# Four fused graph layers on one core: where the last group's row work stands in the first stripe of a pair layer

## The chip, the core and the metric

The kernel runs on one core of a Trainium2 chip. A core has TensorE (PE, whose weight loads are shown as PEld), VectorE (DVE), ScalarE (ACT), GpSimd (POOL) and the queue engine SyncE (SP). The metric is the device time of one execution in microseconds, as the median of several runs. A profile is one execution, recorded by the hardware.

## The reference, cut to what matters

There are N = 4096 nodes of D = 64 features and a dense 0/1 matrix `adj` of 4096 x 4096. Four layers follow each other, each ending in a layer norm of x plus the layer's result.

```python
# layer 0: mean over neighbours, linear, relu, unit length
h = (adj @ X + X) / (sum(adj, 1) + 1)
z = relu(concat(X, h) @ W + b); out = z / norm(z)
# layers 1 and 3: attention over all pairs in hyperbolic space
x_t = logmap0(x)
adj_att = sigmoid(x_t @ w_l [:, None] + x_t @ w_r [None, :] + b) * adj
support = einsum('ij,ijd->id', adj_att, logmap(x[:, None], x[None, :]))
out = proj(expmap(x, support))
# layer 2: sum over neighbours, weighted by 0.5 ** (neighbours still to come)
out = w @ (x @ weight) + bias
# after each
x = layernorm(x + out)
```

## The kernel before, in words

**Tiling.** The target nodes are cut into four stripes of 1024 (`NW`, `WW`), the same 1024 nodes are also a *group* of eight blocks of 128 (`WB`). `GROUPS` is 3, 2, 1, 0 and `BLOCKS` is 31 down to 0, so group 0 is the last group in everything. A layer goes stripe by stripe, and within a stripe over the 32 source blocks in 16 pairs `g`, each with one load of 1 MB of edges (`load`, tile `edges`, six buffers, SP's queue). So all of `adj` is read once a layer.

**Layer 0.** For each stripe four PSUM accumulators (`sums` twice, `counts` twice, name `acc`, six buffers in pool `m0_ps`) collect `adj @ x` in bf16 parts (L1598). DVE checks on part of the edges that they are 0 or 1 (L886). At the end of a stripe the accumulators are copied to SBUF (L1628, L1636), in the last stripe two by ACT and two by DVE.

**Row work.** What is done once per node is written as Python generators that run in steps between the big instructions. `later` puts one on a queue, `tick(n)` moves time on by n and steps what is due, and a generator yields how many ticks it wants to wait: `soon`, `near`, `after` and `far` work these out; `far(small, large)` counts POOL's small and large operations. `need(tag)` ticks until some generator has finished. For group s after layer 0 the row work is:

- `end_0`: the sums per node (L1544, L1545, PE, into an auxiliary bank `aux` and, where there is one, a spare bank), division by the degree (L1550 to L1553), relu (L1557), squares on POOL (L1559), the norm (L1561, L1562).
- `norm_rows`: mean (L939, L940), variance (L951, L953), one over its root.
- `prepare`: 1 - c |x|^2 and its reciprocal (L974, L977), `y`; then its second half, `second()`: casts into `ys` and `yd` (L986 to L1002), the factor of the logarithm (L1015 to L1053, root `rt`), four transposes (L1040, copied by L1044 into `hi_lo`, `src`, `lo_hi`, `dst`), the products with the attention vectors (L1057), `left` and `right` (L1080 to L1082), and some checks (`good`).

For the last group (`pooled`) most small operations run on POOL. `Small(True, "").rsqrt` is one DVE step (L787) and some ten POOL steps (L791 to L802). ACT takes its logarithms with two activations (L1052, L1053).

**Pair layers (1 and 3), `attend`.** For each block j and stripe s three matmuls per half fill a PSUM tile `z` of two banks, three buffers (L1170, L1173, L1176); ACT makes a sigmoid from `left_b` and `right` (L1190) and a square (L1193); DVE multiplies (L1196, one per block) and combines (L1199, one per two blocks); PE adds up over j (L1148). The accumulator is copied out by L1211. The first stripe of layer 1 begins while group 0 still lacks its row work: `end_0(0)` is queued at its start, and `need((layer, 2 * g // WB))` holds the program order back when the stripe reaches the blocks of group 0, its last four pairs `g`. In layer 3 the same happens behind `end_2`. In the first stripe a block pair has 6 ticks in layer 1 (`rate` 2) and 12 in layer 3 (`rate` 4).

**Order.** In layers 0 and 2 PE and ACT issue in the order in which the program is written (`manual_schedule`). Otherwise a planner in the compiler picks, by its own costs, among what it takes to be ready, in program order. `add_manual_dep` ties one instruction's place in the order behind another's, without a wait. In all but the first stripe of a layer `mark` ties row work on PE, ACT and DVE behind the pairs written before it (`pairs_last`). In first stripes nothing ties it.

Of the kernel before, what the change touches and what calls it, by code (L numbers as in the profile page):

```python
# [10 lines left out]
F32 = mybir.dt.float32  # L11
# [50 lines left out]
def gnn_stack_kernel(  # L62
# [509 lines left out]
    def stream(fits):  # L572

        with ExitStack() as st:
# [23 lines left out]
            pairs_last, seen, anchored = {}, [0], [False]  # L598

            def mark(rows):  # L600
                traced = nc.cur_bb.bb.instructions
                for i in traced[seen[0] :]:
                    if i.engine not in ROW_ENGINES:
                        continue
                    if not rows:
                        pairs_last[i.engine] = i
                    elif anchored[0] and i.engine in pairs_last:
                        tc.add_manual_dep(
                            i, pairs_last[i.engine].name,
                            mybir.DependencyInfo(  # L610
                                mybir.DependencyClass.NoSync, mybir.DependencyReason.DATA
                            ),
                            reason="row work behind the pairs",
                        )
                seen[0] = len(traced)

# [319 lines left out]
            def norm_rows(layer, s, v, x2_to):  # L936

                m, v2, sq = nums("n_m"), nums("n_v2"), grp("sq")
                V.tensor_reduce(m, v, AX.X, ALU.add)  # L939
                V.tensor_scalar(m, m, 1.0 / D, None, ALU.mult)  # L940
                pooled = s == GROUPS[-1]
                E = nc.gpsimd if pooled else V
# [8 lines left out]
                V.tensor_reduce(v2, sq, AX.X, ALU.add)  # L951
                yield soon()
                V.tensor_scalar(m, v2, 1.0 / D, 1e-5, ALU.mult, ALU.add)  # L953
                if pooled:
                    r = yield from Small(True, "").rsqrt(m, "n_r", 0)
                else:
# [8 lines left out]
            def prepare(layer, s, att, b_att, curve, least, good, small):  # L965
# [11 lines left out]
                V.reciprocal(rbg, bg)  # L977
# [7 lines left out]
                def second():  # L985
                    nc.scalar.copy(ys[:, :, :D], y)  # L986
# [27 lines left out]
                    q, q1, t = nums("q"), nums("q1"), nums("tt")  # L1014
                    V.tensor_scalar(q, x2[:, at], least, c, ALU.max, ALU.mult)  # L1015
                    V.tensor_scalar(q1, q, SMALL, None, ALU.max)
                    if pooled:
                        rt = yield from Small(True, "").rsqrt(q1, "rt", 0)
                    else:
                        rt = rsqrt(q1, "rt")  # L1020
# [33 lines left out]
                    yield from free()  # L1054
                    p = take(F32, P, WB, 7)
# [868 lines left out]
```

## Time and profile before

| | |
|---|---|
| median of 3 runs | 1049.47 us (1048.6 to 1050.73) |
| the profiled execution, its own time | 1051.42 us |
| its span, first to last instruction | 1049.7 us |
| PE, DVE, ACT, POOL busy | 977.7, 907.8, 751.7, 322.1 us |
| granted PE clock, mean | 0.986 |
| layer 0, until PE's last sums | 0 to 176 us |
| layer 1, first stripe's end (L1211) | 280.7 us |
| layer 1, second and third | 356.5 and 435.3 us |
| layer 3, the four stripes' ends | 798.6, 875.7, 953.9, 1026.7 us |

The page of the profile gives busy times for the whole span, then the span in slices, then the chain of work that ended last and the costliest groups of instructions. Lines of the order of time read: start in us, length in us, engine, line, operation, output and inputs with their shapes, and in square brackets how long the engine had stood before and what ended that. A length is until the result is written, so neighbours overlap.

### The profile page before, as it was taken

Reading aid. Unit: us, or ns where it says so; the run is one execution under the profiler, and the core shown is the slowest. Engines: PE = TensorE matmul, PEld = TensorE weight load, DVE = VectorE, ACT = ScalarE, POOL = GpSimd, SP = SyncE. Lnnn points to the kernel's source line nnn. Section 1 sums busy time; section 2 is a strip of 40 time slices with the busy share of each in tenths; the row PEclk is TensorE's granted clock in tenths of the full one; section 3 lists DMA queues with packets and bytes.
Section 4 is the critical chain, followed back from the end, with each engine's and each line's share of the span. In section 5 each row is a group of like instructions: output and inputs, shape, how many; then the busy total and the mean of one; then the engine's idle time right before and its main releaser. Section 6 shows DMA issues by size and latency. Waiting matters only on the chain.

```text
span 1049.7 us, 13606 instructions
## 1 busy us (share of the span) xinstructions
PE 977.7 (93%) x4845; PEld 397.9 (38%) x4845; DVE 907.8 (86%) x1401; ACT 751.7 (72%) x873; POOL 322.1 (31%) x695
## 2 busy tenths in 40 slices
PE   5999997979999999999999999998999999999991
PEld 2455554423333333333333344443333333333330
DVE  7486978789999999999488579858999999999996
ACT  0003123769989888898677688888998898888970
POOL 0011111163055365365210020104501662572660
PEclk9999999999999999999999999999999999999996
DMA  8999999655665566566599998996465666665600
GB/s 339 421 416 407 394 422 381 228 189 177 235 233 203 206 240 208 193 241 229 213 327 353 369 358 308 327 332 231 168 233 199 241 210 205 241 229 186 233 1 24
DMA packets 38580, 271.62 MB, mean 259 GB/s; under 512 B 4710, under 2 KB 4710, under 8 KB 5734
## 3 DMA queue, kind: packets, MB, share of 16 engines
q1 hardware_dynamic: 37728, 270.03, 70.0%
q8 instruction: 40, 0.66, 0.2%
q10 hardware_dynamic: 774, 0.63, 0.2%
q14 instruction: 38, 0.31, 0.1%
HBM read 269.58 MB, written 1.05 MB: 258 GB/s over the span
## 4 chain that ended last, share of the span: by engine, by line
PE 60%; DVE 22%; DMA 6%; POOL 5%; ACT 4%; issue 2%; ACTq 0%; SPq 0%; POOLq 0%; DVEq 0%
PE acc L1148 16%; PE z L1790 11%; PE z L1170 8%; DVE t L1199 7%; PE z L1176 7%; PE z L1173 7%; DVE t L1196 6%; DMA edges<-in_adj_dram 5%; PE z L1802 3%; DVE junk L886 3%; PE acc L1598 3%; PE z L1756 2%; ACT sq L1193 2%; ACT sq L1797 1%; DMA w_twice<-in_L_gnn_weight_dram 1%
## 5 line engine op out<-in xcount | busy, mean ns | idle before, releaser
L1196 DVE SCALAR_TENSOR_TENSOR t<-z,sig 128x1024 f32<-128x1024 f32 x256 | 308.6, 1218 | 24.9 <-ACT sq L1193 22.7
L1193 ACT ACTIVATE sq<-z 128x1024 f32<-128x1024 f32 x256 | 255.5, 1023 | 66.0 <-PE z L1176 31.9
L1199 DVE SCALAR_TENSOR_TENSOR t<-sq,t 128x2048 f32<-128x2048 f32 x127 | 294.5, 2319 | 0.3
L1190 ACT ACTIVATE sig<-left_b,right 128x1024 f32<-128x1024 f32 x256 | 287.0, 1149 | 1.9 <-DVE t L1196 1.0
L1148 PE MATMUL acc<-t,xe 128*64 128x512 f32 x1024 | 255.7, 605 | 16.0 <-DVE t L1199 14.7
L1170 PE MATMUL z<-edges,two_i 128*128 128x512 bf16 x512 | 201.1, 393 | 1.1 <-DVE t L1196 1.1
L1176 PE MATMUL z<-dst,src 74*128 74x512 f16 x512 | 195.1, 381 | 0.0
L1173 PE MATMUL z<-lo_hi,hi_lo 128*128 128x512 f16 x512 | 194.0, 379 | 0.0
L1797 ACT ACTIVATE sq<-z 128x512 bf16<-128x512 f32 (+1 forms) x192 | 138.0, 740 | 39.9 <-PE z L1790 38.7
L1148 PEld LDWEIGHTS acc<-t,xe 128*64 128x64 f32 x1024 | 63.6, 136 | 145.0 <-issue 104.3
L886 DVE SCALAR_TENSOR_TENSOR t<-edges 128x2048 bf16<-128x2048 f32 x36 | 82.4, 2304 | 19.7 <-DMA edges<-in_adj_dram 19.5
L1598 PE MATMUL acc<-edges,first 128*128 128x512 bf16 x256 | 80.2, 394 | 20.5 <-DMA edges<-in_adj_dram 20.0
L1170 PEld LDWEIGHTS <-two_i 128*128 128x128 bf16 x512 | 50.4, 98 | 119.9 <-issue 74.7
L1790 PE MATMUL z<-edges,pass_by 128*128 128x512 bf16 x248 | 86.6, 389 | 6.3 <-ACT sq L1797 5.7
L1790 PE MATMUL z<-edges,enter 128*128 128x512 bf16 x256 | 88.3, 387 | 0.0
L1598 PE MATMUL acc<-edges,third 128*65 128x512 bf16 x256 | 79.5, 391 | 0.0
L1176 PEld LDWEIGHTS <-src 74*128 74x128 f16 x512 | 49.2, 96 | 72.6 <-issue 10.6
L886 DVE SCALAR_TENSOR_TENSOR junk<-edges 128x2048 bf16<-128x2048 f32 x28 | 64.0, 2284 | 11.7 <-DMA edges<-in_adj_dram 11.6
L1173 PEld LDWEIGHTS <-hi_lo 128*128 128x128 f16 x512 | 50.3, 98 | 56.6 <-issue 11.3
L1299 POOL TENSOR_TENSOR w_att<-x,u 128x512 f32<-128x512 f32 x6 | 16.2, 2707 | 149.5 <-ACT u L1293 149.5
L1756 PE MATMUL z<-sq,halves 128*128 128x512 bf16 x128 | 48.0, 377 | 0.2 <-ACT sq L1797 0.2
L1404 ACT COPY x_t<-aux 64x512 f32<-64x512 f32 x8 | 4.6, 576 | 57.5 <-PE aux L1399 57.5
(476 smaller groups left out, 989.4 us busy)
## 6 DMA issues: line engine op xcount, KB each, us to landing
edges<-in_adj_dram SPq DMA_DIRECT2D x256, 1024.0 KB, 4.9
x<-in_x_dram SPq DMA_DIRECT2D x4, 256.0 KB
out_dram<-x ACTq DMA_DIRECT2D x2, 256.0 KB
out_dram<-x SPq DMA_DIRECT2D x2, 256.0 KB
w_sb<-in_L_gnn_W_dram ACTq DMA_DIRECT2D x1, 32.0 KB, 4.8
w_twice<-in_L_gnn_weight_dram ACTq DMA_DIRECT2D x2, 16.0 KB, 7.9
given<-in_L_gnn_b_dram ACTq DMA_DIRECT2D x1, 0.2 KB
given<-in_L_gnn_bias_dram ACTq DMA_DIRECT2D x1, 0.2 KB
```

Source lines behind the costliest of these rows:

```text
L886: V.scalar_tensor_tensor(junk, a, 0.0, a, ALU.not_equal, ALU.not_equal, accum_out=odd[:, n : n + 1])
L1148: it = nc.tensor.matmul(acc[h * D : (h + 1) * D, :], xe[:, j, :], t[:, k, h * W : (h + 1) * W], start=j == BLOCKS[0], stop=j == BLOCKS[-1],)
L1170: nc.tensor.matmul(half, two_i, edge[:, at : at + W], start=True, stop=False)
L1173: nc.tensor.matmul(half, hi_lo[:, of], lo_hi[:, to], start=False, stop=False)
L1176: last = nc.tensor.matmul(half, src[:, of], dst[:, to], start=False, stop=True)
L1190: nc.scalar.activation(sig, left_b, AF.Sigmoid, bias=right[:, j : j + 1])
L1193: nc.scalar.activation(sq[:, k], zp, AF.Square, bias=ROOT + OFF, scale=-1.0 / UNIT)
L1196: V.scalar_tensor_tensor(ts[k][:, k], zp, 0.0, sig, ALU.max, ALU.mult)
L1199: V.scalar_tensor_tensor(t, sq, HIGH**2, t, ALU.add, ALU.mult)
L1598: nc.tensor.matmul(accs[h][:m], lhs[:, j, :], edge[:, at : at + W], start=j == BLOCKS[0], stop=j == BLOCKS[-1],)
L1790: nc.tensor.matmul(z[:, h : h + W], lhs, rhs[:, h : h + W], start=j == BLOCKS[0], stop=True, skip_group_check=True,)
L1797: weighed[0] = nc.scalar.activation(w, z[:, :n], AF.Exp, bias=-(OFF_EDGE + CUT) * LN2, scale=-LN2)
```

## The change

- In layer 0 two accumulator tiles are taken and given back (a one-element memset each) ahead of the first stripe, which turns the rotation of the buffers.
- The first sigmoid of layer 1's first stripe is issued in the last stripe of layer 0, before its last ticks, into a buffer of `lefts`. The one-element sigmoid `turned_on`, which loaded the table there, is gone.
- In the last stripe of layer 0 each pair `g` has 5 ticks, not 4.
- In `end_0`, when it runs in layer 1, the first matmul of each half of the sums per node is tied behind the pair matmuls written before it.
- A context `burst` ties the DVE instructions written in it, for the last group: the first one behind the latest pair step of DVE, and the next three pair steps behind its last one. It stands around the division and relu, the norm, the mean, the variance and the reciprocal. In `end_0` there are longer waits (4 ticks ahead of the division, `far(0, 1)` ahead of the norm); one `soon()` between two steps of the variance is gone.
- The two steps that prepare `rt` (L1015, L1016) stand in the burst with the reciprocal, and `rt` itself is computed at the start of `second()`, ahead of the casts. Ahead of the products with the attention vectors the last group waits 2 ticks more.
- `norm_rows` and `prepare` serve layers 1 and 3, so the bursts in them apply to both.

```diff
+            DVE, ahead = mybir.EngineType.DVE, []
+            def in_order(one, behind):
...
             def mark(rows):
...
                     if not rows:
                         pairs_last[i.engine] = i
+                        if i.engine == DVE and ahead:
+                            in_order(i, ahead.pop())
...
+            @contextmanager
+            def burst(on):
+                traced = nc.cur_bb.bb.instructions
+                start = len(traced)
+                yield
+                ours = [i for i in traced[start:] if i.engine == DVE]
+                if on and ours:
+                    if DVE in pairs_last:
+                        in_order(ours[0], pairs_last[DVE])
+                    ahead[:] = [ours[-1]] * 3
...
+                with burst(pooled):
+                    V.tensor_reduce(m, v, AX.X, ALU.add)
+                    V.tensor_scalar(m, m, 1.0 / D, None, ALU.mult)
...
+                with burst(pooled):
+                    V.tensor_reduce(v2, sq, AX.X, ALU.add)
+                    if not pooled:
+                        yield soon()
+                    V.tensor_scalar(m, v2, 1.0 / D, 1e-5, ALU.mult, ALU.add)
+                    if pooled:
+                        r = yield from Small(True, "").rsqrt(m, "n_r", 0)
...
+                qs = [nums(n + "_0") for n in ("q", "q1")] if pooled else []
+                with burst(pooled):
+                    V.reciprocal(rbg, bg)
+                    if pooled:
+                        V.tensor_scalar(qs[0], x2[:, at], least, c, ALU.max, ALU.mult)
+                        V.tensor_scalar(qs[1], qs[0], SMALL, None, ALU.max)
...
                 def second():
+                    if pooled:
+                        rt = yield from Small(True, "").rsqrt(qs[1], "rt", 0)
                     nc.scalar.copy(ys[:, :, :D], y)
...
                     yield from free()
+                    if pooled:
+                        yield 2
+                        yield from free()
                     p = take(F32, P, WB, 7)
...
+            def sigmoid(layer, s, j):
+                early = layer == 1 and j == BLOCKS[0] and s == GROUPS[0]
+                if early:
+                    sig = lefts.tile([P, WW], F32, name="left_b")
+                else:
+                    sig = sb.tile([P, WW], F32, name="sig", bufs=3)
+                nc.scalar.activation(sig, left_bs[s], AF.Sigmoid, bias=right[:, j : j + 1])
+                return sig
...
+                        sig = ahead_of.pop() if ahead_of else sigmoid(layer, s, j)
...
+                                if place[0] == 1 and not k:
+                                    in_order(one.ins, pairs_last[mybir.EngineType.PE])
...
+                        pooled = s == GROUPS[-1]
+                        if pooled:
+                            yield 4
+                        with burst(pooled):
...
-                    V.tensor_scalar(z, z, 0.0, None, ALU.max)
...
-                    yield 1
-                    V.tensor_reduce(n2, sq, AX.X, ALU.add)
-                    V.tensor_scalar(n2, n2, 1e-24, None, ALU.max)
-                    if s == GROUPS[-1]:
-                        n = yield from Small(True, "").rsqrt(n2, "n", 0)
+                    yield far(0, 1) if pooled else 1
+                    with burst(pooled):
+                        V.tensor_reduce(n2, sq, AX.X, ALU.add)
+                        V.tensor_scalar(n2, n2, 1e-24, None, ALU.max)
+                        if pooled:
+                            n = yield from Small(True, "").rsqrt(n2, "n", 0)
...
+                        if s == GROUPS[0]:
+                            for _ in range(2):
+                                V.memset(ps.tile([P, W], F32, name="acc")[:1, :1], 0.0)
...
-                            tick(4)
+                            if last and g == 0:
+                                ahead_of.append(sigmoid(1, GROUPS[0], BLOCKS[0]))
+                            tick(5 if last else 4)
...
-                        if last:
-                            nc.scalar.activation(turned_on, one_row[:, :1], AF.Sigmoid)
```

## The prediction

> **What bounds the kernel now.** I read the stages first (busy time by window), then the eight times at which a stripe's accumulator is copied out (line L1211), then the waits and the order of time around the worst stage.
>
> ```profile
> 188.00:254.00 66.00, 58.75 (x302) 23.08 (x300) 58.39 (x75) 54.62 (x58) 30.16 (x56) 1.00 0.55 192
> 254.00:281.00 27.00, 26.36 (x120) 9.70 (x119) 25.95 (x21) 26.43 (x29) 0.00 (x0) 1.00 0.61 216
> 281.00:357.00 76.00, 76.00 (x338) 27.09 (x336) 74.99 (x55) 68.21 (x73) 35.20 (x88) 1.00 0.64 223
> ```
>
> Columns after the length: busy us of PE, PEld, DVE, ACT, POOL, then clock and DMA. In a settled stripe (third row) PE is busy all 76 us: PE sets the pace, with DVE close behind. In the first stripe of layer 1 (rows one and two) neither is full. The copies L1211 come at 280.7, 356.5 and 435.3 us, so settled stripes take 75.8 and 78.8 us; the first one takes 280.7 - 183.65 (its first pair matmul) = 97.1 us. In layer 3 the first stripe goes from its first L1196 at 709.0 to 798.6 us, 89.6, and the next takes 77.1. So some 18 us and 12 us lie in the two first stripes, the ones the change touches. Where they go, at the seam:
>
> ```profile
> 176.18 0.34 PE L1057 MATMUL aux<-att,hi_lo 128*128 128x7 bf16 x8
> 180.63 0.66 PE L1544 MATMUL aux<-sum_w,sums 128*128 128x65 f32 x2 [4.11 <-DVE own L1070]
> ...
> 183.65 0.63 PE L1170 MATMUL z<-edges,two_i 128*128 128x512 bf16 x1
> ```
>
> PE stands 4.11 us (the sums per node need an auxiliary bank that DVE still reads), then computes half of those sums, then the first pairs. The first pair step of DVE, L1196, comes at 187.56. And inside the stripe:
>
> ```profile
> 211.00 0.69 DVE L939 TENSOR_REDUCE n_m<-z 128x8 f32<-128x512 f32 x1 [2.26 <-POOL z L1566]
> 211.61 2.28 DVE L1199 SCALAR_TENSOR_TENSOR t<-sq,t 128x2048 f32<-128x2048 f32 x1
> 213.81 0.16 DVE L940 TENSOR_SCALAR n_m<-n_m 128x8 f32<-128x8 f32 x1
> 213.88 1.22 DVE L1196 SCALAR_TENSOR_TENSOR t<-z,sig 128x1024 f32<-128x1024 f32 x1
> 216.31 0.69 DVE L951 TENSOR_REDUCE n_v<-sq 128x8 f32<-128x512 f32 x1 [1.21 <-POOL sq L945]
> ```
>
> The last group's chain of small steps goes back and forth between DVE and POOL. Its DVE links come too early (DVE stands 2.26 and 1.21 us) or are cut by a 2.2 us L1199. Its last link, L1082 `right`, ends at 253.1 us; four of the stripe's sixteen block pairs need it.
>
> **What the Trainium skill says.** "TensorE: Matmul & The Clock Gate", Part 1: after an idle window of about 3.4 us the PE clock is halved, until a similar window of work has passed. The trace agrees: after the 4.11 us the clock is half until about 187.4 us, and start to start of a pair matmul is 0.43 us, not 0.22. "SBUF — State Buffer", section "SBUF: two separate sides": DVE and GpSimd share a port pair as an exclusive lock, which a DVE operation with two SBUF inputs takes for its whole length. The trace fits it: POOL L801 takes 0.20 us at 208.01 and 2.13 at 222.86, beside L1199 (0.196 to 2.279 us over its 23 runs). "ScalarE: Activation LUTs", "What ACT_TABLE_LOAD costs": a load takes 1.283 us; here L1623's took 1.28.
>
> **The change part by part.**
>
> *Rotation.* The banks are those of the program of before. The last stripe of layer 0 sits in banks 2, 5 (`sums`) and 6, 3 (`counts`); the first `z` of layer 1 covers 2 and 3. So it waits for `sums[0]` (ACT) and `counts[1]` (DVE, L1636, ended 179.7). Banks are given out in the order in which they came free; with two taken and returned at the start, I work out 6, 3 and 4, 1: the first `z` waits for one DVE copy, `sums[1]`, the next two for ACT alone. The two memsets cost about 0.06 us each, before x has landed (DVE idles 2.07 us there for it): nothing.
>
> *tick(5).* The row work of group 1 starts its second half 48 ticks into the last stripe: 12 block pairs at four ticks, 9.6 at five. At 2.45 us a pair (edges come at that pace) that is 5.9 us earlier. DVE's run of small steps, from 171.06 to 181.2 with the copies near its end, then ends near 175, and the copies follow PE's last sums (176.0) at once: `sums[1]` by 176.8. Cover: layer 0 waits for edges; transposes that come early could make PE wait, and six load buffers at 2.45 us hide up to about 12 us of that. Cost 0; without the cover 1 us.
>
> *Sums behind the pairs.* The first `z` need not stand behind L1544: 176.8 instead of 183.65. PE idles under 1 us, so the clock stays whole. Six matmuls at 0.22 give the first L1196 at 176.8 + 1.4 = **178.2 instead of 187.56: 9.4 us**. The sixteen small fp32 pairs then follow two `z` (16 x 0.22 = 3.5 us), beside 2 x 1.13 + 2.2 = 4.5 us of DVE work that is ready: nothing, 3.5 us if DVE runs out.
>
> *Early sigmoid.* It takes over the table load (1.28 + 0.20 us at L1623, just ahead of the sums' copies) and one 1.15 us sigmoid, in a stretch where ACT stands 5.84 us for transposes. Nothing is added; the copies start up to 1.5 us earlier, counted above. It waits for `right` and `left_b` of the first group, long done. Behind it in ACT's order stand only copies that wait for PE.
>
> *Bursts and their waits.* The instructions stay; their places become fixed: behind the latest pair step of DVE, and ahead of the next three. The first stripe has 6 ticks a block pair, 72 up to the pair that needs the last group. By the yields of after the chain is: sums at tick 4 to 6, divide and relu +4, norm +7, mean +12, variance +1+8, reciprocal +12, second half +7+1, transposes +13, then two turns of 2, the new 2, and 2: 75 to 79, forced at 72. Before, the same count is about 68, but the trace took 253.1 - 187.56 = 65.5 us, for DVE was not where the plan had it. A pair costs DVE 2 x 1.13 + 2.2 + gaps = 4.54 us, and the small steps some 6 us in twelve pairs: (12 x 4.54 + 6)/72 = 0.84 us a tick. So 178.2 + 72 x 0.84 = 238.7, and about 6 us of links (transposes, copies, Ln with two table loads, products), as the trace took from 247 to 253: `right` near **245, 8 us earlier**. Each link has POOL's time in its wait: variance 9 ticks = 7.6 us for 2.1 us of work, reciprocal 12 = 10 us for 7.2 in the trace with two collisions. So DVE should not stand in a burst. From `right` to L1211 took 27.6 us; four pairs at 4.62 and the drain, with less left over (the turns of group 1 are done by then), I put at 26: **271 instead of 280.7, 9.7 us**. Bounds: no gain if the chain slips by 10 us; 15 us if it never binds, since DVE's own work, 178.2 + 16 x 4.54 + 6 + 3 of drain + 3, ends at 263 to 266.
>
> *rt moved ahead of the copies.* POOL's eleven steps (3.1 us plain, 7.1 in the trace with two collisions) run before rather than behind the copies into `ys`: the Ln at 246.2 waited for them, while the casts wait only for `y`. POOL's later steps (`ys` L996 to L1012, 5 us) come that much later, and the transposes wait for these: 0, between -2 and +3 us. It is inside the bounds above.
>
> *Layer 3.* Same bursts, no new start. There `right` ends at 757.2 and is needed near 775, so the chain does not bind; what can go is DVE's 1.37 us before L977 and some of PE's three waits for L1199 (1.31, 0.62, 1.29). I take **1 us**, between -3 and +3.
>
> Sum: 9.7 + 1 = 10.7 us. The profiled execution took 1051.42 us (span 1049.7), so it would take 1040.7; against the median of 1049.47 shown, **1038.8, say 1039**. What comes after the first stripe is as before: settled stripes are PE's.
>
> **Rivals.** *(a) The chain never binds.* DVE alone sets the first stripe: 15 + 1, so 1033.5. For it: links would have to follow each other as fast as planned. Against: the tick count passes 72.
> *(b) The chain keeps its end.* Earlier start, longer fixed waits: 79 ticks at 0.92 instead of 0.84 bring `right` to 251. Gain 2 + 1: 1046.5. For it: the tick of before was (250 - 187.56)/72 = 0.87.
> *(c) Slower: DVE stands in its bursts.* A burst cannot be passed, so when POOL is late, three pair steps and behind them PE stand. There are five bursts with POOL ahead of them in layer 1 and three in layer 3. Each collision costs POOL 2 us. If the lateness averages above 10.7/8 = 1.3 us a burst, the gain is gone; at 1.9 the time is 1049.5 + 4.5 = 1054. Against: the margins above.
> *(d) The seam does not move.* DVE is still busy with group 1 at 180 and the first `z` waits for its copy. Only the order against L1544 is won, 3 us at half clock: 1046 to 1049.
>
> **How the numbers follow.** Chances: forecast 0.50 (1034 to 1044), (a) 0.14, (b) 0.17, (d) 0.07, (c) 0.12. Leaving out the tails of (a) and (c) gives 1030 to 1049. A measurement of this kernel can tell about 0.2%, 2.1 us, from no change. Faster: forecast, (a), most of (b) and half of (d), 0.82; same 0.07; slower (c), 0.11.
>
> **What would show it.** The first pair matmul near 177 with no half clock at the seam; first L1196 near 178; L1082 of the last group near 245; the first L1211 near 271 and the first of layer 3 about 90 us after its start, or 1 less; 2 us stalls of DVE gone ahead of L939 and L977. It is wrong if the seam is right and L1211 still comes at 278 or later (then b or c: look for DVE waiting for POOL at L1561, L939, L951, L977), or if layer 3's first stripe grows.

## The result, and the profile after

The change makes the kernel slower. Its median is 1059.48 us (1058.44 to 1061.62, 5 runs), beside 1050.40 us for the kernel before (1048.6 to 1051.96): a ratio of 1.0089, 95% interval 1.0075 to 1.0103. The profiled execution spans 1057.4 us, 7.7 more than before (1049.7). Its lines L1223, L1226, L1229, L1241, L1181 are L1193, L1196, L1199, L1211, L1148 of before; L1166 is the sigmoid, L1082 and L1083 are the two Ln.

The busy time by window, with the windows moved to the changed kernel's own stages (columns as before: busy us of PE, PEld, DVE, ACT, POOL, clock, DMA):

```profile
186.00:254.00 68.00, 56.76 (x270) 22.40 (x275) 63.24 (x78) 52.13 (x54) 29.84 (x56) 0.98 0.58 216
254.00:283.00 29.00, 28.02 (x129) 10.54 (x130) 21.01 (x17) 27.12 (x29) 0.00 (x0) 0.94 0.52 181
283.00:360.00 77.00, 76.51 (x338) 27.66 (x343) 76.23 (x57) 69.51 (x74) 35.38 (x88) 1.00 0.65 224
```

In the first row DVE is now busy 63.2 of 68 us (before 58.4 of 66): the first stripe up to `right` is nearer to DVE's bound, yet not shorter. In the second DVE falls to 21.0 of 29 us; before it had 26.0 of 27.

The stages, in us. *First step* is the first pair step on DVE (L1226), *right* the end of the last group's `right`. The last three columns are kernels of the experiments below. Each column is one execution: those of e5 and e8 took 2.3 and 0.5 us more than their medians, that of e11 2.7 us less.

| | before | after | e5 | e8 | e11 |
|---|---|---|---|---|---|
| PE's last sums of layer 0 end | 175.9 | 179.8 | 175.9 | 174.7 | 175.1 |
| first z on PE | 183.65 | 182.88 | 180.59 | 182.20 | 177.44 |
| first step | 187.56 | 185.72 | 184.48 | 186.10 | 180.42 |
| `right` | 253.2 | 254.1 | 252.6 | 252.0 | 245.3 |
| first stripe's sums copied | 280.7 | 283.0 | 278.8 | 277.6 | 271.1 |
| second stripe takes | 75.8 | 77.1 | 77.2 | 77.2 | 75.7 |
| layer 3, first stripe, from first step | 89.6 | 93.1 | 90.35 | 90.4 | 90.7 |
| pair steps on DVE ahead of `right` | 23 | 24 | 24 | 24 | 24 |
| DVE idle from first step to `right` | 7.05 | 4.31 | 4.12 | 2.18 | 1.95 |

So the 7.7 us are 2.3 up to the end of the first stripe, 1.4 in the second, 3.6 in layer 3's first and 0.8 in its other three, less 0.3 elsewhere. Three places of the trace carry it.

**The seam.** The order of time of PE, then of ACT, in the changed kernel:

```profile
170.41 0.62 PE L1070 MATMUL aux<-ident,ys 128*128 128x128 f16 x8 [2.71 <-DVE ys L1031]
...
180.06 0.61 PE L1070 MATMUL aux<-ident,yd 128*74 128x128 f16 x8
182.88 0.39 PE L1203 MATMUL z<-edges,two_i 128*128 128x512 bf16 x1 [2.21 <-ACT w_att L1679]
```

```profile
179.81 1.15 ACT L1166 ACTIVATE sig<-left_b,right 128x1024 f32<-128x1024 f32 x1 [3.04 <-DVE lr L1100]
180.87 0.99 ACT L1074 COPY lo_hi<-aux 128x1024 f16<-128x1024 f16 x1
181.76 0.59 ACT L1671 COPY sums<-acc 128x512 f32<-128x512 f32 x1
182.24 0.59 ACT L1679 COPY w_att<-acc 65x512 f32<-65x512 f32 x1
```

Three pairs before the end of layer 0 PE stands 2.71 us for a row step of group 1, which the fifth tick put ahead of the remaining pairs; at 151.5 us it had stood 1.09 for another row step. The two, 3.8 us together, are the bulk of the 3.9 us by which layer 0 ends later (some 0.7 us of transposes and products that stood behind the last sums now stand ahead of them too, and about 1 us of waits for edges falls away), for nothing hides them: in this stripe PE waits for no edges from 136.8 us on, as in the kernel before from 133.6 to 168.3 (there it then waits 0.53 and 0.51 us for them, without any wait for row work). Then the first z waits for ACT: a second sigmoid stood 3.04 us for group 1's row work, and behind it in ACT's order are `lo_hi` and only then the copies of the sums. The half clock at the seam is gone in this execution (z matmuls follow at 0.22 us), and from the last sums to the first step it is 5.9 us instead of 11.7. Net, the first step is 1.8 us earlier. In the second profile of this kernel (e9) z matmuls follow at some 0.43 us from 183.7 to 186.3, and the first step comes at 187.2, only 0.4 us earlier than before.

**Inside the stripe.** DVE in the changed kernel, the bursts and what stands after them:

```profile
211.20 0.69 DVE L960 TENSOR_REDUCE n_m<-z 128x8 f32<-128x512 f32 x1
...
218.79 0.68 DVE L972 TENSOR_REDUCE n_v<-sq 128x8 f32<-128x512 f32 x1
...
239.73 0.23 DVE L1097 TENSOR_SCALAR m<-b,k_of_y 128x8 f32<-128x8 f32 x1 [2.01 <-POOL xe L1041]
...
258.74 1.23 DVE L1226 SCALAR_TENSOR_TENSOR t<-z,sig 128x1024 f32<-128x1024 f32 x1 [4.57 <-ACT sig L1166]
```

L960 and L972 (before L939 and L951) carry no brackets any more: the 2.26 and 1.21 us are gone, as the bursts intend. New are 2.01 us for POOL, which runs `rt` first and so reads the old `m` later, and 4.57 us for a sigmoid. That last wait does not come from the table loads of the next paragraph alone: kernels with the bursts and only two loads still have 2.6 to 3.2 us of it (e2, e5 to e8, e11, e12), and those without bursts (before, e3, e4, e10) have none.

**The logarithms.** ACT in the changed kernel, squares and sigmoids left out, and under it the same stretch of the kernel before:

```profile
240.22 1.28 ACT L1082 ACT_TABLE_LOAD   x1
244.29 0.21 ACT L1082 ACTIVATE tt<-tt 128x8 f32<-128x8 f32 x1 [2.79 <-POOL tt L1052]
...
245.43 1.28 ACT L1166 ACT_TABLE_LOAD   x1
...
248.69 1.00 ACT L1074 COPY hi_lo<-aux 128x1024 f16<-128x1024 f16 x1
249.71 1.28 ACT L1083 ACT_TABLE_LOAD   x1
251.00 0.21 ACT L1083 ACTIVATE q<-q 128x8 f32<-128x8 f32 x1
...
256.27 1.28 ACT L1166 ACT_TABLE_LOAD   x1
```

```profile
237.85 1.01 ACT L1044 COPY hi_lo<-aux 128x1024 f16<-128x1024 f16 x1
...
244.72 1.28 ACT L1052 ACT_TABLE_LOAD   x1
246.23 0.21 ACT L1052 ACTIVATE tt<-tt 128x8 f32<-128x8 f32 x1 [0.22 <-POOL tt L1022]
...
247.25 0.20 ACT L1053 ACTIVATE q<-q 128x8 f32<-128x8 f32 x1
247.46 1.28 ACT L1190 ACT_TABLE_LOAD   x1
```

Before, the planner put `hi_lo` first, then both Ln between one table load and one back. In the changed kernel the first Ln stands ahead of `hi_lo`: ACT loads the table, stands 2.79 us for POOL, and goes back to the sigmoid's table; after `hi_lo`, copied 10.8 us later than before, the second Ln needs a load of its own and a fourth brings the sigmoid back. PE meanwhile runs dry (busy 2.08 of 5.7 us from 246.0) and its clock is 0.56 in the 6.8 us from 251.7. Layer 3 has the same four loads, at 745.0, 749.1, 756.3 and 759.5 us, with 1.71 us for POOL and `hi_lo` at 752.4 instead of 745.4. I call this *the split Ln*.

### The profile page after: what moved, and what is told of

The parts are those of the page before. It is cut to its first block, busy times and chain, and to the rows that moved or that the text cites. A ratio compares the mean times of both kernels' runs of the same rounds, so it can differ in the third digit from the quotient of the medians.

```text
span 1057.4 us, 13525 instructions
## 1 busy us (share of the span) xinstructions
PE 974.0 (92%) x4760; PEld 399.0 (38%) x4845; DVE 909.3 (86%) x1403; ACT 758.0 (72%) x876; POOL 317.5 (30%) x695
## 4 chain that ended last, share of the span: by engine, by line
PE 54%; DVE 15%; ACT 5%; issue 1%; POOL 1%; ACTq 0%; POOLq 0%; DVEq 0%
PE acc L1181 16%; PE z L1833 11%; PE z L1206 7%; DVE t L1229 7%; PE z L1209 7%; PE z L1203 6%; DVE t L1226 6%; PE z L1845 3%; PE z L1799 2%; ACT sq L1223 2%; ACT sq L1840 1%; PE aux L1312 1%; ACT sig L1166 1%; PE aux L1147 1%; PE aux L1070 0%
## 5 line engine op out<-in xcount | busy, mean ns | idle before, releaser
L1226 DVE SCALAR_TENSOR_TENSOR t<-z,sig 128x1024 f32<-128x1024 f32 x255 | 306.6, 1217 | 27.4 <-ACT sq L1223 20.6
L1223 ACT ACTIVATE sq<-z 128x1024 f32<-128x1024 f32 x256 | 255.2, 1021 | 64.0 <-DVE t L1229 28.6
L1229 DVE SCALAR_TENSOR_TENSOR t<-sq,t 128x2048 f32<-128x2048 f32 x127 | 296.3, 2333 | 0.5
L1166 ACT ACTIVATE sig<-left_b,right 128x1024 f32<-128x1024 f32 x255 | 286.0, 1149 | 6.3 <-DVE lr L1100 3.0
L1181 PE MATMUL acc<-t,xe 128*64 128x512 f32 x1024 | 257.2, 611 | 15.6 <-DVE t L1229 15.0
L1203 PE MATMUL z<-edges,two_i 128*128 128x512 bf16 x463 | 180.9, 391 | 5.7 <-DVE t L1226 3.5
L1181 PEld LDWEIGHTS acc<-t,xe 128*64 128x64 f32 x1024 | 64.2, 137 | 145.0 <-issue 106.9
L1833 PE MATMUL z<-edges,enter 128*128 128x512 bf16 x248 | 85.9, 387 | 0.5
L1799 PE MATMUL z<-sq,halves 128*128 128x512 bf16 x122 | 45.7, 377 | 0.5 <-ACT sq L1840 0.2
```

The lines of the kernel that those rows point to most:

```text
L1166: nc.scalar.activation(sig, left_bs[s], AF.Sigmoid, bias=right[:, j : j + 1])
L1181: it = nc.tensor.matmul(acc[h * D : (h + 1) * D, :], xe[:, j, :], t[:, k, h * W : (h + 1) * W], start=j == BLOCKS[0], stop=j == BLOCKS[-1],)
L1203: nc.tensor.matmul(half, two_i, edge[:, at : at + W], start=True, stop=False)
L1223: nc.scalar.activation(sq[:, k], zp, AF.Square, bias=ROOT + OFF, scale=-1.0 / UNIT)
L1226: V.scalar_tensor_tensor(ts[k][:, k], zp, 0.0, sig, ALU.max, ALU.mult)
L1229: V.scalar_tensor_tensor(t, sq, HIGH**2, t, ALU.add, ALU.mult)
```

## The experiments

All ratios are to the kernel before, run beside each group on the same chip (medians 1050.3, 1049.5 and 1049.9 us), with 95% intervals. Single executions of these kernels scatter by up to some 10 us, and the longer ones have the lower granted clock (in e1 the fastest of 12 took 1050.8 us at a mean of 0.988, the slowest 1064.1 at 0.975); so the medians tell the size and the profiles the place.

| run | kernel | median us | ratio |
|---|---|---|---|
| e9 | changed kernel again | 1058.24 | 1.0077 (1.0056 to 1.0098) |
| e1 | changed, four ticks | 1057.32 | 1.0069 (1.0046 to 1.0092) |
| e2 | changed, Ln together | 1051.91 | 1.0016 (1.0002 to 1.0029) |
| e3 | changed, no bursts | 1060.36 | 1.0106 (1.0077 to 1.0136) |
| e4 | before, seam's edits alone | 1055.60 | 1.0057 (1.0036 to 1.0078) |
| e5 | e2 and four ticks | 1048.90 | 1.0001 (0.9988 to 1.0015) |
| e6 | e5, ScalarE's copies | 1047.89 | 0.9989 (0.9977 to 1.0002) |
| e7 | e5, short waits | 1048.17 | 0.9986 (0.9968 to 1.0004) |
| e8 | before, row work's edits, Ln together | 1051.09 | 1.0019 (1.0009 to 1.0029) |
| e10 | e4 with four ticks and ScalarE's copies | 1050.59 | 1.0008 (0.9996 to 1.0020) |
| e11 | e5, ScalarE's copies and short waits | 1045.12 | 0.9960 (0.9945 to 0.9976) |
| e12 | e11, layer 3's row work as before | 1043.35 | 0.9942 (0.9922 to 0.9961) |

My theory from the result's trace was: the split Ln and the fifth tick make the loss. The main rival: the bursts with their fixed places do.

### The two Ln together (e2), and the changed kernel again (e9)

```diff
-                        nc.scalar.copy(into[:, cols], turned[:n])
+                        turns_made.append(nc.scalar.copy(into[:, cols], turned[:n]))
...
-                        nc.scalar.activation(t, t, AF.Ln, bias=1.0)
-                        nc.scalar.activation(q1, q1, AF.Ln, bias=1.0, scale=-1.0)
+                        one = nc.scalar.activation(t, t, AF.Ln, bias=1.0)
+                        two = nc.scalar.activation(q1, q1, AF.Ln, bias=1.0, scale=-1.0)
+                        if pooled:
+                            in_order(one.ins, turns_made[0].ins)
+                            in_order(two.ins, one.ins)
```

`turns_made[0]` is the copy of `hi_lo`. So the tie does two things, which no run takes apart: it keeps the two Ln together, and it lets `hi_lo` go first.

> The changed kernel with one tie more in the last group's row work: the first Ln is issued on ScalarE behind the copy of hi_lo, and the second behind the first with only the copy of src and one square between them, so that each first stripe has one table load for Ln and one back, where the changed kernel has two of each. Theory (the planner set the first Ln ahead of hi_lo's copy, where ScalarE stood 2.8 us for POOL in layer 1 and 1.7 us in layer 3, and split the two Ln): hi_lo is copied some 8 us earlier, two loads of 1.28 us go in each first stripe, the first stripe of layer 1 goes from 97.3 us (first pair step to the copy of the sums) to 91 to 94, that of layer 3 from 93.1 to 89 to 91, and the whole is 5 to 9 us shorter: 1050 to 1054 us. Rival (the chain is bound by POOL's and VectorE's links, and ScalarE's wait only moves): right is written within 1 us of where it is now in both stripes, and the whole is 0 to 3 us shorter: 1056 to 1059 us.

> The changed kernel once more, beside the others of this study on one chip. It should be 0.7 to 1.0% slower than the kernel before, and 0.6 to 0.8% slower than the kernel with both Ln tied alone if the tie's gain of 7.6 us is real; if the two were only measured on different chips, it comes out within 0.3% of the kernel before.

Measured: 1051.91 us, and the changed kernel beside the last group again 1.0077. The tie is worth 0.61 to 0.73% of the time, 6.4 to 7.7 us: the theory's side. Layer 3 shows it plainly. ACT there in e2, squares and sigmoids left out:

```profile
750.33 1.00 ACT L1076 COPY hi_lo<-aux 128x1024 f16<-128x1024 f16 x1
...
753.19 1.28 ACT L1084 ACT_TABLE_LOAD   x1
754.49 0.21 ACT L1084 ACTIVATE tt<-tt 128x8 f32<-128x8 f32 x1
...
755.50 0.21 ACT L1085 ACTIVATE q<-q 128x8 f32<-128x8 f32 x1
755.72 1.28 ACT L1171 ACT_TABLE_LOAD   x1
```

There are two loads, and the first stripe falls from 93.1 to 90.3 us. It takes 90.3 to 90.7 us in every profile with the tie there (e2, e5 to e8, e11) and 93.1 to 94.8 in all with the split (after, e9, e1, e3).

In layer 1 the profiles don't settle the size. This execution of e2, the slowest of its 22 (1057.7 us), had layer 0 end at 182.4 us and half clock at the seam, and its stripe took 96.7 us, as the rival wanted, with `right` 70.5 us after the first step. e5, which has the same tie, takes 94.3 us. With the split it is 97.3 us in the changed kernel, and 95.7 in e9, which has the same four loads in both stripes. So the profiles show 2.8 us in layer 3 and at most some 3 in layer 1; the rest of the medians' difference lies in executions of which there is no profile.

### Four ticks in layer 0's last stripe (e1), and both mends (e5)

```diff
-                            tick(5 if last else 4)
+                            tick(4)
```

> The changed kernel with one edit undone: tick(4) again after each pair of layer 0's last stripe; rotation, early sigmoid, sums behind the pairs, bursts and the rt move stay. Theory (the fifth step brings row work of group 1 in front of the last pairs, and TensorE stands 2.7 us at 170.4 us for a VectorE copy three pairs before the end, too late to catch up): the last sums of layer 0 end within 1 us of the kernel before (176.0 us, against 179.8 in the changed kernel), the first stripe of layer 1 keeps its 97 us, and the whole is 3 to 4 us shorter than the changed kernel: 1055 to 1057 us, ratio to the kernel before near 1.005. Rival (layer 0 ends later because of the swapped banks or the sigmoid in ACT's fixed order, or only because the loads ran behind): the last sums still end near 179 us and the whole stays within 1 us of 1059.5. Second rival (group 1's row work then falls into the first stripe of layer 1 and pushes that one back): layer 0 ends near 176 us, but the stripe behind it takes 100 us and the whole is unchanged.

> The changed kernel with both Ln of the last group tied together behind the copy of hi_lo, and with four ticks again in layer 0's last stripe. If the split Ln (7.6 us of the medians) and the fifth step (2.2 us) add up, the whole is 1049 to 1050.5 us, no slower than the kernel before; layer 0 ends near 175.7 us and layer 3's first stripe takes 90 us. Rival (the fifth step's time is paid back at the seam, where the sums' VectorE copies then stand behind group 1's row work and the first z waits 4 us for them): 1051.5 to 1053 us, as with the tie alone.

Measured: in e1 layer 0 ends at 175.7 us, so the fifth tick is what made it late (the five profiles with it end layer 0 at 179.4 to 182.4 us; of the nine with four ticks eight end it at 174.7 to 175.9, e7's at 178.1). But the second rival has a part too: e1's PE, then its DVE, at the seam:

```profile
180.40 0.61 PE L1203 MATMUL z<-edges,two_i 128*128 128x512 bf16 x1 [4.04 <-DVE u L1679]
```

```profile
178.98 0.17 DVE L1111 TENSOR_TENSOR f<-f,m 128x8 f32<-128x8 f32 x1
179.07 0.68 DVE L1671 COPY sums<-acc 128x512 f32<-128x512 f32 x1
179.67 0.68 DVE L1679 COPY u<-acc 65x512 f32<-65x512 f32 x1
```

This profile is the slowest of e1's 12 (1064.1 us), but e5's has the same wait (4.05 us). Group 1's row work now ends at 179, DVE's two copies of the sums stand behind it, and the first z waits 4.04 us. Most of what layer 0 gains is lost again, and that idle time brings back the half clock. The whole is 1057.3 us, 0.9 to 2.2 us below the changed kernel's two medians, and the intervals overlap: alone it is not shown to help. With the tie as well (e5) it is 1048.9 us, 0.1 below the range expected: by the ratios 1.6 us below e2 and 8 to 9 below the changed kernel. The loss is gone, ratio 1.0001.

### The bursts: taken out of the changed kernel (e3), and the row work's edits without the seam's (e8)

e3 replaces `with burst(pooled)` by `with burst(False)` and takes back `yield 4` and `far(0, 1)`. e8 has tie, bursts, waits and the `rt` move, and none of the seam's edits.

> The changed kernel with the bursts and the longer waits that came with them undone (each small VectorE step is issued where the kernel before had it, far(0,1) is 1 again and the 4 ticks behind the sums per node go); rotation, fifth step, early sigmoid, sums behind the pairs, rt ahead of the copies and the 2 ticks ahead of the products stay. In layer 1 the copies of hi_lo and src stand ahead of both Ln in ScalarE's order, with one load each way; in layer 3 the Ln stay split by four loads. Theory (the split Ln and ScalarE's wait for POOL make the stripes longer, not the bursts): layer 1's first stripe falls from 97.3 to about 92 us, layer 3's stays at 93, and the whole is 4 to 6 us shorter than the changed kernel: about 1054 us. Rival (the bursts themselves, with their longer waits and POOL's operations thrown beside the large VectorE steps, make both stripes longer): both stripes come back to the kernel before, 93 and 89.5 us, and the whole is 7 to 8 us shorter: about 1052 us. Third case (the bursts did help as predicted and something else hides it): both stripes grow by 5 us or more, and the whole is 1065 us or more.

> The kernel before with the row work's edits alone (bursts and their waits, rt ahead of the copies, 2 ticks ahead of the products) and both Ln tied together; no rotation, four ticks, no early sigmoid, sums per node in the kernel before's place. If the bursts bring what the idle time of VectorE ahead of right allows (7.05 us in layer 1's first stripe of the kernel before, of which the changed kernel has 4.3 left; 4.3 against 4.0 us in layer 3), less the one pair step by which right stands later: layer 1's first stripe 91 to 94 us, layer 3's 90.3, the whole 1048 to 1051 us, no change against the kernel before. Rival A (the bursts and waits are a loss by themselves, and the seam's edits a gain that hides it): 1053 us or more. Rival B (the seam's edits are the loss, 5.3 us when they were made alone, and the bursts a gain): 1046 us or less.

Measured: e3 is 1060.4 us; none of its three cases. Its two stripes took 97.8 and 93.4 us. In layer 1 the Ln do stay together and `hi_lo` is copied at 236.3 us, but DVE stands 12.1 us ahead of `right` instead of 4.3, and ACT stands 3.44 us for POOL between the table load and the first Ln. So without the bursts the chain is longer by itself, and taking them out of this kernel wins nothing. Layer 3 shows which edit splits the Ln where: bursts gone, four loads still, from 743.1 to 757.4 us. There the split comes from what e3 keeps: the `rt` move, the two ticks ahead of the products, or the `soon()` that is gone; in layer 1 it comes with the bursts or their longer waits, which e3 takes out together. With none of these (e4) both stripes have two loads.

e8 is 1051.1 us, 1.0019: between its cases, nearest the first. The bursts take DVE's idle time ahead of `right` from 7.05 to 2.18 us. But `right` now stands behind 24 pair steps and 12 of the large step that combines them (L1229 of the changed kernel), where it stood behind 23 and 11, and the large one takes 2.39 us each instead of 2.28. So `right` comes 65.9 us after the first step, as before (65.7). The first stripe wins 1.7 us, the second gives back 1.4 and layer 3's first 0.8.

### The seam's edits alone (e4), and mended (e10)

e4 is the kernel before with rotation, fifth tick, early sigmoid and the tie of the sums per node. e10 has four ticks and the mended copies of e6 below.

> The kernel before with the edits at the seam alone: rotation, fifth step in layer 0's last stripe, early sigmoid, sums per node behind the first pairs; no bursts, rt and q where they were, no ticks ahead of the products. Theory: layer 0 ends near 179.8 us as in the changed kernel (the fifth step), the first pair steps follow 6 us later, near 186, and since both Ln stay together the first stripe of layer 1 takes about as long as before plus the few us by which the row work of the last group now starts later against the first pair step: 93 to 97 us; layer 3 is as before, 89.6 us; the whole is 0 to 3 us from the kernel before: 1048 to 1053 us. Rival (the seam's gain of 5.6 us can never be kept, because the last group's chain sets the end of the stripe and starts with the sums): the copy of the first stripe's sums lands 3 to 4 us later than before, at 284 us, whatever the first pair step gained, and the whole is 1053 to 1055 us.

> The kernel before with the seam's edits alone (rotation, early sigmoid, sums per node behind the first pairs), four ticks, and the last sums copied by ScalarE alone; row work as in the kernel before, both Ln together by the planner's own order. Theory (of the 5.3 us that the seam's edits cost alone, layer 0's late end made some 5 and VectorE's wait for POOL the rest, 13.5 us idle ahead of right against 7.1): first pair step near 180.5 us instead of 187.2, and the whole 1048 to 1051 us. Rival (with the seam's edits POOL's steps fall beside VectorE's large ones whenever the first step comes, and eat what was won): VectorE's idle time ahead of right stays at 12 us or more, the first stripe takes 98 us or more, and the whole is 1050 to 1053 us, though the first step comes 7 us earlier than in the kernel before.

Measured: e4 1055.6 us, the rival's side, for two reasons. Layer 0 ends at 180.8 us, so the first step comes at 187.15, hardly earlier than before (187.56). And the stripe from there takes 98.5 us instead of 93.2. DVE in e4, then POOL in e4:

```profile
211.52 0.69 DVE L960 TENSOR_REDUCE n_m<-z 128x8 f32<-128x512 f32 x1 [4.01 <-POOL z L1596]
...
229.78 0.20 DVE L1000 RECIPROCAL rb<-b 128x8 f32<-128x8 f32 x1 [2.23 <-POOL b L996]
```

```profile
198.10 2.95 POOL L1587 TENSOR_TENSOR sq<-z 128x512 f32<-128x512 f32 x1 [26.37 <-DVE z L1582]
...
205.41 2.20 POOL L816 TENSOR_SCALAR rs_t<-rs_t 128x8 f32<-128x8 f32 x1
```

POOL's squares take 1.04 us alone and 2.95 here, beside DVE's large step; its small step 0.24 and 2.20. Between 196 and 227 us five POOL steps are held so in e4, one in the kernel before. DVE waits 13.5 us ahead of `right` instead of 7.05. But held steps alone do not decide: the changed kernel has four between 196 and 227 us, and no wait of DVE stands ahead of its bursts.

In e10 the first step comes at 180.9 us, 6.6 earlier than before, and yet the time is the same, 1.0008: it is not the late end of layer 0 alone that eats the gain. Its profiled execution is one of its slowest (1056.4 us; median 1050.6). DVE stands 18.7 us in it, 4.3 of them in 13 us of half clock behind the seam (0.53 by the windows) and 6.8 in its waits for POOL ahead of the mean, the variance and the reciprocal (4.8 before); `right` ends at 257.2 us, 4 later than before. So the rival's numbers for DVE and the stripe (103.6 us) came, and the earlier start brought nothing. Its mechanism did not come: five POOL steps up to `right` are held in e10, as many as before, and one of them between 196 and 227 us. That the phase against DVE's large steps decides in e4 is a reading of its trace; no run changed the phase alone, and for e10 the cause stays open.

### Mends: ScalarE's copies (e6), short waits (e7), both (e11), and layer 3 as before (e12)

```diff
-                            copy = V.tensor_copy if last and h else nc.scalar.copy
+                            copy = nc.scalar.copy
...
-                        if pooled:
-                            yield 4
...
-                    if pooled:
-                        yield 2
-                        yield from free()
```

The first line is e6's, the others e7's; e11 and e12 have all. e12's bursts, `rt` move and tie are in layer 1 alone.

> As the kernel with both Ln tied and four ticks, and the two VectorE copies of layer 0's last sums go to ScalarE too, so that they stand behind no row work. Theory (the first z waits for the copies: 4.04 us for VectorE with four ticks, 2.21 us for ScalarE with five): layer 0 ends near 175.7 us, the first z starts near 178 us instead of 180.4, the first pair step falls from 184.3 to about 181.5 us, and the whole is 2 to 3 us below that kernel, 1046.5 to 1048.5 us. Rival (the last group's chain, placed by ticks, and the row work of group 1 set the end, so the first pair step alone brings nothing): first z near 178 us, but TensorE or VectorE stands for group 1's row work a step later, and the whole is within 1 us of that kernel.

> As the kernel with both Ln tied and four ticks, without the two waits that were added by count: the 4 ticks between the sums per node and their use, and the 2 ticks ahead of the products of the last group. Theory (in ticks, right stands behind the 24th pair step of layer 1's first stripe where the kernel before had it behind the 23rd, and the chain is as long as its ticks): right moves one or two pair steps forward, to 22 or 23, the stripe is 2.5 to 5 us shorter, layer 3's first stripe 1 us, and the whole 3 to 5 us below that kernel: 1045 to 1047 us. Rival (without the waits VectorE stands in the bursts for TensorE and POOL instead): right at the 23rd step but VectorE's idle time ahead of it grows by 3 us or more from 4.3, and the whole is within 1 us of that kernel or above it.

> The changed kernel with both Ln tied, four ticks, ScalarE's copies and without the two waits by count. If the gains of the copies (0.12%) and of the shorter waits (0.15%) add up: 1045 to 1047.5 us, 0.2 to 0.4% below the kernel before. If the first pair step no longer matters because VectorE stands for the last group's sigmoid afterwards (3.2 us with the short waits): 1047.5 to 1048.5 us.

> As the mended kernel (both Ln tied, four ticks, ScalarE's copies, without the two waits by count), and layer 3's first stripe with its row work as in the kernel before: no bursts, rt behind the copies, no tie. There the stripe takes 89.6 us instead of 90.4, so the whole should be 0.5 to 1 us below the mended kernel, 1044 to 1047 us: bursts cost layer 3 0.8 us. If bursts cost nothing there, the two are equal.

Measured: e6 has the first z at 177.21 us and the first step at 180.25, even earlier than its theory said, and is 1.0 us below e5, as its rival said (the intervals overlap): in the profiles `right` moves from 252.6 to 250.8 us only. In e7 the second stripe falls to 75.7 us, so its 1.4 us more came from the waits by count; the first takes 92.4. The whole is 1048.2 us, a smaller gain than expected; in its profile layer 0 ends at 178.1. `right` stands behind the 24th step here too, with no new wait for POOL ahead of it: the step count does not come from these waits. Together (e11) they give 1045.1 us, 0.40% below the kernel before: by the medians more than the sum of the two, though the intervals don't tell it from the sum. The windows of e11 for the first stripe, and its ACT, PE and DVE at the seam:

```profile
180.40:245.00 64.60, 60.68 (x312) 24.93 (x317) 62.16 (x76) 54.97 (x58) 31.92 (x56) 1.00 0.63 233
245.00:271.00 26.00, 25.55 (x113) 9.31 (x113) 22.66 (x20) 25.44 (x27) 0.00 (x0) 1.00 0.63 218
```

```profile
175.89 0.60 ACT L1679 COPY u<-acc 65x512 f32<-65x512 f32 x1
176.36 1.03 ACT L1076 COPY src<-aux 74x1024 f16<-74x1024 f16 x1
177.27 2.21 ACT L1168 ACTIVATE sig<-left_b,right 128x1024 f32<-128x1024 f32 x2
179.36 1.95 ACT L1225 ACTIVATE sq<-z 128x1024 f32<-128x1024 f32 x2
```

```profile
177.44 0.39 PE L1205 MATMUL z<-edges,two_i 128*128 128x512 bf16 x1 [1.73 <-ACT src L1076]
```

```profile
180.42 1.23 DVE L1228 SCALAR_TENSOR_TENSOR t<-z,left_b 128x1024 f32<-128x1024 f32 x1 [2.12 <-ACT sq L1225]
```

The clock is whole in both windows, DVE is busy 62.2 of 64.6 us, and the first stripe's sums are copied at 271.1 us: the number that the prediction had for the change. That execution took 1042.4 us, though, and e11's median is 1045.1. e12 has the same program up to there; its profile, with half clock for part of the time behind the seam (0.87 from 181 to 194 us, e11's is whole), has its first step at 180.5 and the copy at 274.4. e12 is the fastest, 1043.35 us, ratio 0.9942, against 1.0089 of the change. Its layer 3 takes 89.6 us where e11's takes 90.7. That layer 3 is better without the bursts and the other row edits is shown by the profiles (89.6 us in all four without them: before, e4, e10, e12); by the medians it is not, since the intervals of e11 and e12 overlap.

## Why the prediction was wrong, point by point

The forecast was 10.7 us shorter, with 11 in 100 for slower; the trace is 7.7 longer, the median 9.1. Of the 18.4 us between, 12.0 lie ahead of the first L1241 (271 predicted, 283.0 measured), 1.4 in the second stripe, 4.6 in layer 3's first (1 less predicted, 3.6 more measured), the rest behind it. In the forecast's own terms, the gain was to come almost all from the seam (9.4 us, of which 1.8 came), and the loss came mainly from a term put near nothing, the order on ACT: two table loads were assumed, four came, and the tie alone takes the loss from 0.77 to 0.89% back to 0.16%.

- **tick(5), "Cover ... Cost 0; without the cover 1 us": failed.** I took it that layer 0 waits for edges, and the load buffers for a cover of PE's waits. But in the last stripe the trace of before has no wait for edges from 133.6 to 168.3 us: PE was behind them, and full buffers don't give a late PE its time back. What could be hidden was the 1 us of its two waits at the end; the row steps cost 1.09 and 2.71 us, and layer 0 ended 3.9 us late. (With four ticks, e1 and e5: 175.7 and 175.9 us.)
- **Rotation and early sigmoid, "the first `z` waits for one DVE copy" and "only copies that wait for PE": failed.** z waited for ACT. I looked at what stands behind the early sigmoid, not at the next sigmoid, which stood 3.04 us for group 1 ahead of the copies. I had 2.2 us from last sums to first step; it was 5.9. With copies that stand behind nothing (e6, e11) it is still 5.3: the first z comes 2.35 us after the sums instead of 0.8, behind one more copy of ACT (`src`), and the first step 3.0 us after the first z instead of 1.4. That is a link which I had left out: DVE's step waits until ACT's square has ended, as the last fence above shows.
- **Sums behind the pairs:** right in that PE no longer stands for them. That the clock stays whole at the seam came in this profile and not in e9's. The size was 1.8 us instead of 9.4, for the two reasons above: 7.5 us of the 12. That the first z can come by 177 was true, once ScalarE alone makes the copies: 177.44 in e11, 6.2 us earlier than before.
- **Bursts, 0.84 us a tick:** this part of the sum was nearly right. From first step to `right` I had 66.8 us, and 68.4 was measured; the twelve L1229 took 2.39 us each where L1199 took 2.28, which is 1.3 us of the difference. But 66.8 is more than the 65.7 of before: the sum itself said that bursts lengthen the chain, and all its gain came from the seam. I did not read that off. (The terms of its tick count add to 77 to 79, not 75 to 79; the chain was taken as forced at 72 all the same.) The stalls that they take away are small, 4.9 us of 7.05 in e8, and there the extra pair step and the longer L1229 cost the same.
- **"About 6 us of links ... Ln with two table loads", and rt "0, between -2 and +3": failed.** Four loads. I followed POOL's order and took ACT's as given, but outside layers 0 and 2 the planner chooses it anew, and a moved step can change it far from the edit. The split Ln costs 6.4 to 7.7 us by the medians, most of the loss: with the tie alone (e2) the change is 1.0016, and with four ticks as well (e5) 1.0001. From `right` to the copy I had 26 us; it was 28.9, with 4.57 us of DVE waiting for a sigmoid and 6.8 us of half clock, and 26.6 in e9. e11 has 25.9.
- **Layer 3, 1 us shorter:** 3.6 longer. 2.8 are the split Ln (e5: 90.35) and 0.8 the bursts with the rest of the row edits (e12: 89.6). The range I gave, -3 to +3, was too narrow by half a microsecond.
- **Rival (c)** had the sign, not the mechanism: DVE stands nowhere in a burst. The places that I named for it (ahead of the norm, the mean, the variance, the reciprocal) show no wait. **(b)**, `right` near 251 by longer waits, is nearer (254.1). The waits by count do cost: 1.4 us in the second stripe.
- **What would show it wrong** said: if layer 3's first stripe grows. It did, and it is the cleanest sign, as no edit at the seam reaches it (89.6 us in e4 and e10, as before).

## What to carry to other kernels

When an edit moves one step in a program whose order a planner chooses, read the new order of every engine before costing it, first where an engine pays to change state: two activations of one table that fall apart here cost two loads of 1.28 us, a wait between them and what stands in line behind. The Trainium skill's page "ScalarE: Activation LUTs", section "Table sets: the hidden batching unit", says to batch activation calls by table set; in this kernel a tie in the order of issue (e2) does that. And ask of a wait near the end of a stage how many rounds are left to win it back, and of a chain's new fixed places whether their sum is shorter than what the trace took before.

## What the runs showed of the hardware that I had not expected

- A large POOL operation that meets a running L1229 pays the same as a small one: 128x512 takes 1.04 us alone and 2.95 beside it (e4's squares), a small step 0.24 and 2.20. The price is about 2 us for each operation that meets it, at both sizes. Up to `right` five operations meet one in the kernel before and five in the changed kernel, so what a meeting costs in the end depends on whether DVE waits for that operation.
- DVE pays as well, when POOL was first. L1199 averages 2.28 us ahead of `right` in the kernel before, and its like 2.33 to 2.39 in kernels with bursts, where single ones take up to 3.00 us. Each of these starts while a POOL operation on 128x512 is running. In the fence at the end POOL has 0.82 us to go when L1229 starts, and L1229 takes 0.70 us more than 2.28. From 180 to 830 us the fourteen traces show 110 single ones above 2.35 us, and all fit alike: longer by what was left of POOL's operation, less 0.13 us. POOL's steps of 0.2 us cost DVE nothing in this way. The prediction had priced only what POOL loses.
- A switch of ACT's table cost the load alone: behind the three loads in the changed kernel's first stripe that no other wait follows, the next activation starts 1.29 to 1.30 us after the load's start (249.71 to 251.00). The Trainium skill's page "ScalarE: Activation LUTs", section "What ACT_TABLE_LOAD costs", adds 1.38 us for draining at every switch; no row and no gap here shows it.
- Half clock lasted very differently: at the seam some 3 us in e5 and 6.8 in the kernel before (180.6 to 187.4, twice the window that the prediction took for it), none in the changed kernel's profile (which has 6.8 us of it from 251.7), and some 16 in e1, where behind the wait of 4.04 us the z matmuls follow at 0.43 us from 180.4 to 196.5. Behind the same wait of 2.21 us it is none in the changed kernel's profile and some 3 us in e9's, so the length of the wait alone does not set it. At half clock a matmul takes twice as long, so such a spell can cost up to half its length, an estimate: 2 to 8 us. An earlier first step with half clock behind it can be no gain (e10).

The changed kernel's L983 on POOL and L1229 on DVE, for the second point:

```profile
222.97 1.04 POOL L983 TENSOR_TENSOR x<-z,n_r 128x512 f32<-128x512 f32 x1
...
223.19 2.98 DVE L1229 SCALAR_TENSOR_TENSOR t<-sq,t 128x2048 f32<-128x2048 f32 x1
```
